# Scores and weighted values for two steps at a time, and a quotient whose clamp and products run on GpSimd

## The chip, the cores and the metric

The kernel runs on one core of one Trainium2 chip. The metric is the device time of one execution in microseconds, from the first instruction to the last, as the median of several runs. Five engines of the core work at the same time, each through its own queue of instructions in order: TensorE (PE, matrix products, with its weight loads shown apart as PEld), VectorE (DVE), ScalarE (ACT), GpSimd (POOL) and SyncE (SP, which here only issues DMAs). They meet at semaphores: an instruction at the head of a queue waits there until what it needs is done, and everything behind it waits too. TensorE writes its results into PSUM, of which this kernel lays out eight banks of 512 fp32 values in each of 128 partitions; DVE and ACT read them from there, and in this kernel GpSimd reads and writes SBUF only.

## The reference, cut to what matters

All data is fp32: an input `x` of eight images of 256 channels and 64 by 64 pixels goes through two layers, each added to its own input after a group normalisation.

Layer 0 makes from each pixel's neighbourhood a small hidden vector (1x1 products `w1`, `w2`, a ReLU, `cw1`, a ReLU), from that nine weights per pixel and group (`cw2`), and sums nine shifted copies of the 1x1 product `x3` with them:

```
h = relu(_bn(concatenate([x1, x2u]), ...)); h = relu(_bn(_conv1x1(h, cw1), ...))
w = _conv1x1(h, cw2, cb2).reshape(B, G, K * K, H, W)
out = einsum('bgskhw,bgkhw->bgshw', x3u, w)
```

Layer 1 adds two branches. The first is local attention in four heads: each pixel's query meets the keys of a 7 by 7 window, softmax, and a sum of the values. The second passes the input through two depthwise 3 by 3 convolutions with a ReLU between them, and multiplies it with a sum over nine softmax weights:

```
att = softmax(einsum('bdn,bdkn->bnk', q, uk + upe)); out_att = einsum('bnk,bdkn->bdn', att, uv)
wts = softmax(einsum('oc,bchw->bohw', Wfc, x).reshape(b, C, 9, h, w), axis=2)
out_conv = sum(oc * wts, over the nine)
return rate1 * out_att + rate2 * out_conv
```

Since `oc` is the same for all nine (the same image is convolved nine times), the second branch is `oc` times a quotient. The kernel computes eight exponentials of differences to the ninth and their sum S, clamps t = min(1 + S, 1e37), and takes t times 1 / t.

## The kernel before, in words

**Tiling.** Work goes in bands of 8 rows (512 pixels, `BAND`); 8 bands make an image, 64 bands the input. The main loop runs over g, the band of layer 1, from -12 to 63. Layer 0 runs `AHEAD` = 12 bands ahead in the same loop, so for g < 0 it stands alone (`alone`), and in the last twelve bands layer 1 does. A band has eight steps s: two halves of the channels (`ct`) times four column blocks of 16 pixels (`m`).

**One step of layer 1.** In the order of the program: `score_tile` takes a PSUM tile of two banks (`sco`, one buffer). `weighted_values` (L747) multiplies the probabilities of the step before last with the values, 16 small matmuls of 112 rows by 64 columns, into columns 256 to 383 of the tile's first bank. `scores` (L703) makes the scores of this step, 8 small matmuls of 64 by 64, and DVE adds the mask and takes the maximum (L712). `add_values` (L757) adds the weighted values to the output rows `xr`. `transposed` (L735) transposes the probabilities of the step before through TensorE, and ACT copies them to SBUF (L737). `exponentials` (L720, ACT) and `probabilities` (L727 DVE, L729 ACT) finish this step's softmax. Two `branch_weights` (L825) each make a 128 by 512 product and its exponential (L830, ACT) into a tile `ex` of two halves, and GpSimd adds the tiles of a half-band (L1026). Between them stand the taps of the depthwise convolutions on DVE (L782, L808), and the queries, keys, values and value transposes of coming bands.

**The quotient.** After step 3 of a half-band `dynamic_sum` runs: GpSimd adds the two halves of the last `ex` (L838), five places later DVE clamps the sum (L845) and takes the reciprocal of its first half (L846), three places later of the second (L850), two places later GpSimd multiplies the sum by it, `oc` by that, and adds to `xr` (L855 to L857). The sum lives in the last `ex` tile, of which there are three.

**Layer 0 in the loop.** `small_maps` (L328) makes the small products at step 0, `value_maps` (L369) the large ones, `hidden_maps` the hidden vector (L429) and `tap_weights` (L447) the nine weights, three at a time after steps 1, 3 and 5. Each weight gives a product over 128 by 1040 on DVE (L460) and a sum on GpSimd (L468).

**What sets the order.** The order on each queue is written by hand: the tile framework records instructions as the Python program reaches them. `advance()` counts places, six to a step, and `after(n, f)` runs f n places later. What waits for what follows from the tiles: an instruction waits for the writers of what it reads, and for the readers of the buffer that it overwrites. All PSUM tiles but `sco` (two banks) and `acc` (one bank) turn in one ring `gen` of five banks: products of L825, L369, L637, L658, L563, L607, L735, L447, L429 and L328 take a bank each in the order of the program.

Of the kernel before, what the change touches and what calls it, by code (L numbers as in the profile page):

```python
# [10 lines left out]
F32 = mybir.dt.float32  # L11
# [7 lines left out]
P = 128  # L19
# [20 lines left out]
TG = 3  # L40
# [25 lines left out]
TAPS_AT = (1, 3, 5), (0, 2, 4)  # L66
PRODUCTS_AT = ((1, 2, 7), (1, 2, 5), (1, 2, 7)), ((7, 14, 10), (9, 17, 13), (12, 20, 16))
# [19 lines left out]
def conv_layers_kernel(ctx: ExitStack, tc: tile.TileContext, ins: dict, out: bass.AP):  # L87
# [98 lines left out]
    def layer1_loads():  # L186


        last = w1.tile([P, NCT, 1, C], F32, tag="rec", name="last", bufs=1)
# [35 lines left out]
    def gn_affine(sts, means, name, done):  # L225
# [9 lines left out]
        def group_means(v, k):  # L235
            pg = ps.tile([P, n], F32, name=f"pg_{name}_{k}", tag="gen", bufs=5)
            nc.tensor.matmul(pg, means, v, start=True, stop=True)
            return pg
# [49 lines left out]
    def scaled_weights(b):  # L288
# [3 lines left out]
        def scale(sc, bi):  # L292
            im.w12s = w0.tile([P, NCT, 2 * REL], F32, tag="w12s", name=f"w12s_{b}", bufs=1)
            im.w3s = w0.tile([P, NCT, C], F32, tag="w3s", name=f"w3s_{b}", bufs=1)
            for kt in range(NCT):
                nc.vector.tensor_scalar(im.w12s[:, kt], w12[:, kt], sc[:, kt : kt + 1], None, ALU.mult)
                nc.vector.tensor_scalar(im.w3s[:, kt], w3[:, kt], sc[:, kt : kt + 1], None, ALU.mult)
            after(5, lambda: through(bi))

        def through(bi):  # L300
            pb = ps.tile([P, 1 + NCT], F32, tag="gen", name=f"pb_{b}", bufs=5)
# [18 lines left out]
    def small_maps(b, i):  # L320
# [4 lines left out]
        p12 = ps.tile([P, R // 2, W], F32, tag="gen", name=f"p12_{b}_{i}", bufs=5)  # L325
# [36 lines left out]
    def value_maps(b, i, mt):  # L362
# [4 lines left out]
        p3 = ps.tile([P, BAND], F32, tag="gen", name=f"p3_{b}_{i}_{mt}", bufs=5)  # L367
# [41 lines left out]
    def hidden_maps(b, i, at):  # L409
# [3 lines left out]
        hids = []  # L413

# [8 lines left out]
        def conv(first, last):  # L423
            if first == 0:
                im.ph = ps.tile([P, SR, W], F32, tag="gen", name=f"ph_{b}_{i}", bufs=5)
            for t in range(first, last):
                n = P if t == 0 else 96
                for q in range(NQR):
                    nc.tensor.matmul(  # L429
                        im.ph[q * REL : (q + 1) * REL], c1[:n, t], hids[t][:n, q * SR : (q + 1) * SR],  # L430
                        start=(t == 0), stop=(t == 2),
                    )

        def relu():
            nc.scalar.activation(h2n[i % 2][:, :, :W], im.ph, AF.Relu, bias=bn2b, scale=bn2s)

        hidden(0)
        for n, f in zip(at, (lambda: hidden(1), lambda: conv(0, 2), lambda: hidden(2), lambda: conv(2, 3), relu)):
            after(n, f)

    def tap_weights(b, i, u, alone, at):
# [3 lines left out]
        pw = ps.tile([P, TG, SR * HP], F32, tag="gen", name=f"pw_{b}_{i}_{u}", bufs=5)  # L445
        for j in range(TG):
            nc.tensor.matmul(  # L447
                pw[:, j], c2[:, TG * u + j], h2n[i % 2].rearrange("p r c -> p (r c)"), start=True, stop=True
            )

        def product(j):
            k = TG * u + j
            if alone and j == TG - 1:
# [11 lines left out]
            if alone and j == TG - 1:  # L465
# [11 lines left out]
        def gather(prod):  # L477
            if u == 0:
                im.part = score_tile(f"sum_{b}_{i}").rearrange("p t (s r c) -> p t s r c", r=SR, c=W)
            for t in range(2):  # L480
                nc.tensor.matmul(
                    im.part[:, t], ident, rows(prod)[:, t * SHARE // 2 : (t + 1) * SHARE // 2],
                    start=(u == 0), stop=(u == KK // TG - 1),
# [18 lines left out]
        for j, n in enumerate(at):  # L502
            after(n, lambda j=j: product(j))


    def norm_rows(b):
# [9 lines left out]
        def by_channel(both):  # L516
            pg = ps.tile([P, NCT, 2], F32, tag="gen", name=f"pgc_{b}", bufs=5)
# [33 lines left out]
    def values(b, j, ct):  # L551
# [3 lines left out]
        pv = ps.tile([P, R, W], F32, tag="gen", name=f"pv_{b}_{j}_{ct}", bufs=5)  # L555
# [45 lines left out]
    def value_tile(b, j, u):  # L601
        im = images[b]
        n = min(R, WP - j * R) * KW
        pvt = ps.tile([CHUNK, 2, C], F32, tag="gen", name=f"pvt_{b}_{j}_{u}", bufs=5)
# [22 lines left out]
    def queries(b, i, ct):  # L627
# [7 lines left out]
        pq = ps.tile([P, R, W], F32, tag="gen", name=f"pq_{nm}", bufs=5)  # L635
# [10 lines left out]
    def keys(b, i, ct):  # L646
# [7 lines left out]
        for a in range(first, last, R):  # L654
            n = min(R, last - a)
            pk = ps.tile([P, R, W], F32, tag="gen", name=f"pk_{b}_{i}_{ct}_{a}", bufs=5)
# [37 lines left out]
    def scores(b, i, ct, m, sco):  # L694
# [4 lines left out]
        nm = f"{b}_{i}_{ct}_{m}"  # L699
        for t in range(2):  # L700
            for h in range(2):
                c0 = (2 * m + t) * TQ
                nc.tensor.matmul(  # L703
                    sco[half[t], h, :NKEY], qb[half[h], 2 * m + t].rearrange("p r c -> p (r c)"),
                    kb[half[h], :, c0 : c0 + KW], start=True, stop=True,
                )

# [422 lines left out]
```

## Time and profile before

| | |
|---|---|
| median of 3 runs | 4155.27 us (4154.16 to 4160.41) |
| the profiled execution | 4152.64 us, its span 4150.9 us |
| TensorE busy | 4022.6 us, 97% of the span |
| DVE, ACT, GpSimd busy | 3591.9, 3081.0 and 2923.0 us |
| first L825 product, last one's end | 247 us and 4137 us |
| mean granted TensorE clock | 0.993 of full |

A group of a profile is a line of the program on one engine, with tiles as out<-in, the shape, the number of instructions, then the busy time and the mean of one in ns, and after the second bar the idle time of the engine just before them and what ended it. A matmul in fp32 is shown as two, and matmuls overlap, since their ends are modelled; what one costs the engine is the distance of two starts. The chain is the work that ended last, followed back step by step to what released it. In the timeline equal instructions in a row are merged: start, length from the first start to the last end, count, and in brackets the idle time ahead with its releaser.

### The profile page before, as it was taken

The page shows a single profiled execution, that of the slowest core. Times are in us where ns is not written, and L with a number is a line of the kernel's source. Part 1 is how long each engine was busy: PE and PEld are TensorE (multiplying, and loading weights), DVE is VectorE, ACT ScalarE, POOL GpSimd, SP SyncE. Part 2 cuts the span into 40 slices and gives each one's busy share as a digit, 9 for nine tenths or more (in the row PEclk, how much of TensorE's full clock was granted, in tenths as well). Part 3 has the DMA queues.
Part 4 walks back from the last instruction along what each step waited for, and adds up shares of the span by engine and source line. Part 5 has one row for each costly group of instructions (what it writes and reads, how often), then busy time and mean ns, then how long its engine had stood idle before and what let it go on. Part 6 is the DMA issues. An engine that isn't in the chain of part 4 may idle for free.

```text
span 4150.9 us, 72735 instructions
## 1 busy us (share of the span) xinstructions
PE 4022.6 (97%) x25292; PEld 2126.8 (51%) x25292; DVE 3591.9 (87%) x7248; ACT 3081.0 (74%) x7726; POOL 2923.0 (70%) x1902
## 2 busy tenths in 40 slices
PE   6789999999999999999999999999999999999998
PEld 3345555555555555555555555555555555455554
DVE  5878998899898898889998898888988889977777
ACT  3467778777787777877778777777778777687776
POOL 4767777677786777777777777777777677744554
PEclk8999999999999999999999999999999999999999
DMA  8854234234244233334234234244233233111100
GB/s 226 194 135 111 73 91 109 72 94 109 62 101 107 76 94 98 81 94 109 72 85 118 72 94 105 66 101 106 71 82 99 65 87 85 33 41 39 39 28 21
DMA packets 381264, 367.89 MB, mean 89 GB/s; under 512 B 55648, under 2 KB 282720, under 8 KB 380640
## 3 DMA queue, kind: packets, MB, share of 16 engines
q1 hardware_dynamic: 377568, 358.68, 34.3%
q8 instruction: 200, 3.28, 0.3%
q10 hardware_dynamic: 3328, 4.55, 0.3%
q14 instruction: 168, 1.38, 0.1%
HBM read 261.42 MB, written 101.71 MB: 87 GB/s over the span
## 4 chain that ended last, share of the span: by engine, by line
PE 71%; DVE 14%; POOL 6%; ACT 5%; DMA 2%; issue 2%; SPq 1%; POOLq 0%; ACTq 0%; DVEq 0%
PE pf L825 33%; PE ptp L735 5%; PE sco L747 5%; PE pk L658 5%; PE sco L703 5%; PE p L369 5%; DVE prod L460 4%; PE pq L637 4%; POOL xg L468 3%; PE pvt L607 2%; PE pv L563 2%; DVE acc L808 2%; PE pw L447 2%; DVE acc L782 2%; POOL ex L1026 2%
## 5 line engine op out<-in xcount | busy, mean ns | idle before, releaser
L825 PE MATMUL pf<-yp,c_wfc 128*128 128x512 f32 x4096 | 1930.5, 595 | 10.6 <-ACT vc L581 5.0
L468 POOL TENSOR_TENSOR xg<-xg,prod 128x1024 f32<-128x1024 f32 x549 | 1203.9, 2193 | 96.6 <-DVE prod L460 64.1
L825 PEld LDWEIGHTS pf<-yp,c_wfc 128*128 128x128 f32 x4096 | 729.9, 190 | 690.5 <-issue 619.4
L1026 POOL TENSOR_TENSOR ex<-ex,ex 128x1024 f32<-128x1024 f32 x384 | 907.7, 2364 | 61.9 <-ACT ex L830 57.2
L830 ACT ACTIVATE ex<-pf 128x512 f32<-128x512 f32 x1024 | 607.3, 593 | 297.9 <-POOL ex L1026 141.3
L782 DVE SCALAR_TENSOR_TENSOR acc<-yp,c_chan,acc 128x504 f32<-128x504 f32 (+3 forms) x1104 | 766.2, 694 | 42.3 <-ACT acc L773 21.7
L460 DVE SCALAR_TENSOR_TENSOR prod<-pw,c_par,x3q 128x1040 f32<-128x1040 f32 x576 | 733.9, 1281 | 66.8 <-PE pw L447 21.6
L808 DVE SCALAR_TENSOR_TENSOR acc<-hid,c_chan,acc 128x504 f32<-128x504 f32 (+3 forms) x1024 | 757.8, 740 | 20.2 <-ACT acc L802 2.1
L855 POOL TENSOR_TENSOR ex<-ex,rec 128x512 f32<-128x512 f32 x127 | 162.3, 1278 | 809.5 <-DVE rec L850 767.1
L729 ACT ACTIVATE prob<-prob,tot 128x196 f32<-128x196 f32 x1024 | 411.6, 450 | 387.2 <-DVE tot L727 386.4
L712 DVE CUSTOM_DVE_ANT_0 prob<-sco,c_mask 128x196 f32<-128x196 f32 x1024 | 325.5, 355 | 272.4 <-PE sco L703 272.0
L720 ACT ACTIVATE prob<-prob,nmax 128x196 f32<-128x196 f32 x1024 | 461.4, 454 | 46.9 <-DVE nmax L712 45.3
L747 PEld LDWEIGHTS sco<-pt,vt 112*64 112x64 f32 x8160 | 283.8, 137 | 182.3 <-issue 51.7
L737 ACT COPY pt<-ptp 112x512 f32<-112x512 f32 x511 | 297.0, 581 | 105.0 <-PE ptp L735 103.0
L735 PE MATMUL ptp<-ident,prob 128*112 128x128 f32 x2044 | 341.7, 287 | 31.2 <-ACT prob L729 30.5
L747 PE MATMUL sco<-pt,vt 112*64 112x64 f32 x8160 | 347.0, 227 | 0.0
L735 PEld LDWEIGHTS ptp<-ident,prob 128*112 128x112 f32 x2044 | 203.9, 133 | 201.4 <-issue 77.7
L703 PE MATMUL sco<-kb,qb 64*64 64x196 f32 x4096 | 295.2, 357 | 0.0
L563 PE MATMUL pv<-yp,c_wv 128*128 128x512 f32 (+2 forms) x576 | 247.3, 554 | 0.6
L369 PE MATMUL p<-xc,w3s 128*128 128x512 f32 x512 | 244.4, 601 | 0.0
L658 PE MATMUL pk<-yp,c_wk 128*128 128x512 f32 (+2 forms) x576 | 240.8, 545 | 0.0
L637 PE MATMUL pq<-yp,c_wq 128*128 128x512 f32 x512 | 240.6, 592 | 0.0
(140 smaller groups left out, 5294.0 us busy)
## 6 DMA issues: line engine op xcount, KB each, us to landing
x<-x3n SPq DMA_DIRECT2D x128, 264.0 KB, 2.1
x3q<-x SPq DMA_DIRECT2D x128, 264.0 KB, 7.2
xc<-in_x SPq DMA_DIRECT2D x64, 512.0 KB, 5.0
xg<-in_x SPq DMA_DIRECT2D x256, 128.0 KB, 4.8
x<-xg SPq DMA_DIRECT2D x256, 128.0 KB, 2.4
yp<-x SPq DMA_DIRECT2D x128, 256.0 KB, 3.3
xr<-x SPq DMA_DIRECT2D x64, 512.0 KB, 5.8
out_x<-xr SPq DMA_DIRECT2D x64, 512.0 KB, 3.1
```

Of the source, the lines that this page charges most:

```text
L369: nc.tensor.matmul(p3, im.w3s[:, kt, mt * P : (mt + 1) * P], im.xc[i][:, kt, :], start=(kt == 0), stop=(kt == NCT - 1),)
L460: nc.vector.scalar_tensor_tensor(prod[:, :, :RUN], pw[:, j, :RUN].unsqueeze(1).to_broadcast([P, SHARE, RUN]), par[:, PCB2 + k : PCB2 + k + 1],
L468: nc.gpsimd.tensor_add(im.xg[i], im.xg[i], rows(prod))
L703: nc.tensor.matmul(sco[half[t], h, :NKEY], qb[half[h], 2 * m + t].rearrange("p r c -> p (r c)"), kb[half[h], :, c0 : c0 + KW], start=True, ...
L720: nc.scalar.activation(prob[:, h, :NKEY], prob[:, h, :NKEY], AF.Exp, bias=nmax[:, h : h + 1], scale=-1.0, accum_out=tot[:, h : h + 1],)
L735: nc.tensor.transpose(ptp[:, h, ch], prob[:, h, ch * CHUNK : (ch + 1) * CHUNK], ident)
L747: nc.tensor.matmul(po[half[h], :, t * TQ : (t + 1) * TQ], im.vt[i + ch, m][:n, t, (2 * ct + h) * HD : (2 * ct + h + 1) * HD], pt[:n, h, ch ...
L782: nc.vector.scalar_tensor_tensor(o, yp[:, ct, ra + dr : rb + dr, ca + dc : cb + dc], chan[:, ct, CW1 + k : CW1 + k + 1], o, ALU.mult, ALU.add,
L808: nc.vector.scalar_tensor_tensor(o, hid[:, ra + dr : rb + dr, ca + dc : cb + dc], chan[:, ct, CW2 + k : CW2 + k + 1], o, ALU.mult, ALU.add,)
L825: nc.tensor.matmul(pf, wfc[:, kt, 2 * m + j, ct * P : (ct + 1) * P], images[b].yp[i][:, kt, PAD : PAD + R], start=(kt == 0), stop=(kt == N ...
L830: nc.scalar.activation(ex[:, j].rearrange("p (r c) -> p r c", r=R), pf, AF.Exp)
L1026: after(4, lambda ex=ex, exb=exb: nc.gpsimd.tensor_add(ex, ex, exb))
```

## The change

The change has five parts.

1. `gen` shrinks from five banks to four. The freed bank is a tile `small` of its own with one buffer. It takes the weighted values of two steps (columns 0 to 255), and in its other half the results of `small_maps` and of the hidden vector.
2. Scores and weighted values are made in every second step, for two steps: 16 score matmuls into a `sco` tile that holds both steps side by side, then up to 32 matmuls of weighted values, then the small products if there are any, then the transposes. In the odd step only the transposes remain; they stand after the first L825 product. `masked` is the part of `scores` that runs on DVE, once in each step as before; the two `add_values` come together.
3. While layer 1 runs, `tap_weights` makes two weights at a time, after steps 1 to 5, and the DVE products follow one and two places later. Before, the third product of a group came seven places later.
4. While layer 1 runs, the hidden vector is summed in two pieces: the first sum is copied to SBUF by ACT in step 4, the second added by DVE in step 6, and then the ReLU. When layer 0 stands alone the sum stays in PSUM, in the bank `acc`.
5. In `dynamic_sum` the sum has a tile of its own, and GpSimd does the clamp. The reciprocal is taken in halves at places 7 and 11, into a tile of half the size, and GpSimd multiplies each half one place later; the rest follows at place 13.

```diff
-TG = 3
+TG = 2, 3
...
-TAPS_AT = (1, 3, 5), (0, 2, 4)
-PRODUCTS_AT = ((1, 2, 7), (1, 2, 5), (1, 2, 7)), ((7, 14, 10), (9, 17, 13), (12, 20, 16))
+TAPS_AT = (1, 2, 3, 4, 5), (0, 2, 4)
+PRODUCTS_AT = ((1, 2),) * 5, ((7, 14, 10), (9, 17, 13), (12, 20, 16))
...
-        p12 = ps.tile([P, R // 2, W], F32, tag="gen", name=f"p12_{b}_{i}", bufs=5)
+        p12 = home[:, 2 * P :].rearrange("p (r c) -> p r c", r=R // 2)
...
+        def one(home):
+            ph = conv(home, 0, 2, 0, 1)
+            after(1, lambda: hidden(2))
+            after(2, lambda: nc.scalar.copy(h2, ph))
+
+        def two(home):
+            ph = conv(home, 2, 3, 2, 2)
+            after(1, lambda: nc.vector.tensor_add(h2, ph, h2))
+            after(3, lambda: relu(h2))
...
-        pw = ps.tile([P, TG, SR * HP], F32, tag="gen", name=f"pw_{b}_{i}_{u}", bufs=5)
-        for j in range(TG):
+        first, n = TG[alone] * u, min(TG[alone], KK - TG[alone] * u)
+        pw = ps.tile([P, n, SR * HP], F32, tag="gen", name=f"pw_{b}_{i}_{u}", bufs=4)
+        for j in range(n):
...
+    def score_of(sco, h, m):
+        return sco[:, h, m % 2 * NKEY : (m % 2 + 1) * NKEY]
...
-        po = sco[:, 0, 256 : 256 + 2 * NQ].rearrange("p (r c) -> p r c", r=R)
+        po = po[:, m % 2]
...
+    def small_tile(nm):
+        return ps.tile([P, 4 * P], F32, tag="small", name=f"small_{nm}")
+
+    def weigh_steps(steps, home):
+        po = home[:, : 2 * P].rearrange("p (s r c) -> p s r c", s=2, r=R)
+        return [(a, weighted_values(*a, pt, po)) for a, pt in steps]
...
-        tot = ex[:, 1]
+        tot = w1.tile([P, BAND], F32, tag="tots", name=f"tot_{b}_{i}_{ct}", bufs=1)
...
-        engine.tensor_add(tot, tot, ex[:, 0])
-        rec = w1.tile([P, BAND], F32, tag="rec", name=f"rec_{b}_{i}_{ct}", bufs=1)
-        n = BAND // 2
-
-        def quotient():
-            nc.vector.tensor_scalar(tot, tot, 1.0, 1.0e37, ALU.add, ALU.min)
-            nc.vector.reciprocal(rec[:, :n], tot[:, :n])
-            after(3, second)
-
-        def second():
-            nc.vector.reciprocal(rec[:, n:], tot[:, n:])
-            after(2, weigh)
+        engine.tensor_add(tot, ex[:, 1], ex[:, 0])
+        engine.tensor_scalar(tot, tot, 1.0, 1.0e37, ALU.add, ALU.min)
+        rec = w1.tile([P, BAND // 2], F32, tag="rec", name=f"rec_{b}_{i}_{ct}", bufs=1)
+
+        def quotient(u):
+            v = tot[:, u * BAND // 2 : (u + 1) * BAND // 2]
+            nc.vector.reciprocal(rec, v)
+            after(1, lambda: engine.tensor_mul(v, v, rec))
...
-            engine.tensor_mul(tot, tot, rec)
             engine.tensor_mul(oc, oc, tot)
...
-        after(5, quotient)
+        after(7, lambda: quotient(0))
+        after(11, lambda: quotient(1))
+        after(13, weigh)
...
-                    sco = score_tile(nm)
-                    weighted = [(a, weighted_values(*a, pt, sco)) for a, pt in pending]
-                    prob, nmax = scores(b, i, ct, m, sco)
+                    weighted = []
+                    if m % 2 == 0:
+                        sco = score_tile(nm)
+                        for e in range(2):
+                            scores(b, i, ct, m + e, sco)
+                        small = small_tile(nm)
+                        weighted, pending = weigh_steps(pending, small), []
+                        if s == 0 and g + AHEAD < B * NB:
+                            mid.append(small_maps(*divmod(g + AHEAD, NB), small))
+                        if s in (4, 6) and convs:
+                            convs.pop()(small)
+                        if before is not None:
+                            pending.append((before[:-1], transposed(nm, before[-1])))
+                    prob, nmax = masked(nm, m, sco)
                     for a, po in weighted:
                         add_values(*a, po)
-                    pending = [] if before is None else [(before[:-1], transposed(nm, before[-1]))]
                     tot = exponentials(nm, prob, nmax)
                 advance()
                 if g >= 0:
                     ex, exb = w1.tile([P, 2, BAND], F32, tag="ex", name=f"ex_{nm}", bufs=3), ex if m else None
                     branch_weights(b, i, ct, m, 0, ex)
+                    if m % 2:
+                        pending.append((before[:-1], transposed(nm, before[-1])))
```

All other tiles of the ring have `bufs=4` in place of `bufs=5`. The tile that takes the last ninth of the `wfc` weights at the start uses the buffers of `oc` in place of those of `rec`.

## The prediction, made before the changed kernel ran

> **What bounds the kernel now.** First the page: busy time, and the chain that ended last.
>
> ```profile
> PE 4022.6 (97%) x25292; PEld 2126.8 (51%) x25292; DVE 3591.9 (87%) x7248; ACT 3081.0 (74%) x7726; POOL 2923.0 (70%) x1902
> ...
> PE 71%; DVE 14%; POOL 6%; ACT 5%; DMA 2%; issue 2%; SPq 1%; POOLq 0%; ACTq 0%; DVEq 0%
> ```
>
> TensorE carries most of the chain, but 97% busy isn't 97% at its rate. So I took the distances of starts. Four matmuls of 512 columns take 1.72 us (0.429 each). Summing such medians per group over the main loop (247 to 4137 us), I find about 140 us of TensorE time above a normal pass. About half are waits of over 0.15 us; the rest is small variation. In a common band (61.6 us; there are 64 bands, those that start an image take 68.8) 59.5 us are work at its normal pitch, 2.1 are lost. That is all that removing waits can win.
>
> The rest must come from the work. The timeline of TensorE in one step:
>
> ```profile
> 2004.92 1.88 PE L369 MATMUL p<-xc,w3s 128*128 128x512 f32 x4
> 2006.73 0.69 PE L747 MATMUL sco<-pt,vt 112*64 112x64 f32 x16
> 2007.34 0.58 PE L703 MATMUL sco<-kb,qb 64*64 64x196 f32 x8
> 2007.85 0.65 PE L735 MATMUL ptp<-ident,prob 128*112 128x128 f32 x4
> 2008.34 1.88 PE L825 MATMUL pf<-yp,c_wfc 128*128 128x512 f32 x4
> ```
>
> L369 should hand over at 2004.92 + 1.72 = 2006.64; L747 starts at 2006.73. By the starts of the single matmuls, a pair of L747 takes 0.0585 us, the first one 0.106; four of L703 take 0.226; the transposes 0.109 each. So a step loses 0.094 entering L747, 0.048 in its first pair, 0.101 going to L703, 0.054 going back to full width: 0.297 us, eight times a band, with nobody to wait for.
>
> Then the waits. A common band stalls at its end; the timelines of TensorE and DVE and the chain of that stretch:
>
> ```profile
> 2053.44 0.78 PE L735 MATMUL ptp<-ident,prob 128*112 128x128 f32 x4 [0.34 <-ACT prob L729]
> ```
> ```profile
> 2008.82 0.41 DVE L845 TENSOR_SCALAR ex<-ex 128x512 f32<-128x512 f32 x1
> ...
> 2039.47 2.38 DVE L845 TENSOR_SCALAR ex<-ex 128x512 f32<-128x512 f32 x1 [0.43 <-POOL ex L838]
> ```
> ```profile
> 2048.14 1.20 DVE prod L460
> ...
> 2052.92 0.81 ACT prob L729 x2
> 2053.73 0.58 ACT qb L641
> 2054.32 0.04 issue
> 2054.36 1.98 PE pf L825 x4
> ```
>
> TensorE waits for a bank and a probability, both behind ACT, behind DVE, which is late. One DVE clamp took 2.38 us beside GpSimd's L468 (2039.39 for 2.17 us), and 0.41 with GpSimd idle.
>
> **What the Trainium skill says.** "TensorEngine Tiling (Array Packing)", Key Properties: changing the tiling mode drains TensorE, changing the tile doesn't. The trace agrees: 0.05 to 0.1 us at each change of shape above, none between transposes and L825. "SBUF — State Buffer", Who interferes with whom: a `tensor_scalar` of DVE in its two-port mode and a GpSimd operation exclude each other for a whole instruction. The 2.38 against 0.41 us fit. "GPSIMD Engine Reference", Elementwise — side-by-side cycle accounting: short bodies with one input take 1.03 cycles per element there, with two inputs about 2.6. In the trace a GpSimd copy of 420 columns takes 534 ns, an addition of 512 1272 ns.
>
> **The change part by part.** *Pairs.* Two steps cost 2 x (0.297 + 0.468 + 0.452 + 0.049 + 0.437) = 3.41 us before (eight pairs of L747, two fours of L703, the first transpose's 0.049 extra, four transposes). Afterwards: changes once, 0.297; scores 4 x 0.226 = 0.904; values 16 x 0.0585 = 0.936; transposes 0.049 + 2 x 0.437 = 0.923; sum 3.06. The odd step's transposes stand between full-width products, so they change no mode. Gain 0.345 us per pair, four pairs, 64 bands: **-88 us**. The small products keep their changes: they leave from full width and come to narrow before, the reverse after. I didn't see scores follow full width in a steady band, so a change may cost 0.05 or 0.12: -60 to -105. Matmul counts are unchanged (the nine weights are nine twice 0.113 either way).
>
> *The wait for scores.* DVE's L712 waits 272.0 us for L703 over the run. In odd steps its scores are there. This idle time isn't TensorE's; it lets DVE start early, which counts below.
>
> *Clamp and halves.* DVE loses 128 x 1070 ns = 137 us, and gains 53 small additions of 128 by 128 (0.3 us as L757, 16 us). GpSimd gains 127 clamps; from the copy's 1.27 ns per column 0.65 us (from 0.44, an estimate by that page's 1.03 cycles at its 1.2 GHz, to 1.27 as the addition): 83 us, and some 0.1 us per quotient for the split: 13 us. GpSimd is then at 3020 us, 74%: not full, but not even over a band. ACT gains 53 copies of 0.3 us, inside its idle time.
>
> *The new waits.* The second reciprocal overwrites the first's tile, so DVE waits for GpSimd's first half product; the first waits for the clamp. I followed GpSimd's new queue with its pitches (L468 2.15, L1026 2.35, L838 1.23, oc 1.35, xr 1.23, kb 0.5, pe 1.1) from the start of step 2, t = 0. The first product ends 1.2, the second 5.4 (behind a reciprocal). From there GpSimd never rests: L468, L1026, a half product, kb, oc, xr to 13.7; two L468 and L1026 to 20.3; two L468 and L1026 to 27.0; the quotient's sum 28.2, its clamp 28.9; two L468 and `pe` 34.3; the half product 34.9. DVE, by its own pitches (product 1.21, mask pair 0.57, reciprocal 1.67, tap 0.72), would be at the first reciprocal at 27.4, so it waits 1.5; the second reciprocal, after taps, a product and masks, would start at 34.3 and waits 0.7. Then 1.67, 0.3 and two taps later the softmax reciprocal ends 38.5, ACT's scaling 39.3, and the query copy (0.57) frees the bank. TensorE, by the pitches above, wants the transposes of step 7 at 39.2 and gets bank and data near 39.9: a stall of 0.7, and perhaps 0.4 at the next bank. That is the 0.85 of before (0.41 + 0.44) plus up to 0.3. The rest of DVE's day is lighter, and the transposes are due 1 to 2 us later in a step.
>
> *Four banks.* The ring loses one, but three tenants go (the small products, hidden vector twice), and a group of weights holds its bank two places, not seven. The closest call is the second L825 of step 3, due at 12.1, whose bank DVE frees at 11.4 with its second product of that step; that of step 5 has 0.9 us. Hidden unless DVE is 0.7 us later; at 1.2 us later about 0.5 us in two places of 52 bands, 52 us.
>
> *Longer hold of `xr`.* The store moves from place 16 to 19 of the quotient, half a step, and the load of the next `xr` follows in step 5 on SP, its first use in step 2: hidden by some 20 us. The stretch before 247 us keeps its order but for the bank of the hidden vector: 0, -5 to +5. The last 14 us: +0.2.
>
> Sum: -88, stalls +15 (0.3 x 51 bands): **-73 us**. Against the profiled execution, 4152.6 - 73 = 4079.6; the median of the runs stands 2.6 higher, so **4082 us**.
>
> **The rivals.** *GpSimd sets the pace* (slower). Place: step 6, DVE's second reciprocal behind GpSimd's half product, behind two L468 and `pe`. It decides when that chain pushes TensorE 1.7 us per band beyond today's stall: 88 us / 52 bands. My walk leaves 1.4 us of room. For it: GpSimd runs without rest for 30 us, and a clamp at 1.27 us adds 0.6 at once. Against: GpSimd's order up to the clamp is nearly that of before, and transposes are due later. At 2.5 us per band: 4155 + 0.8 x 52, about 4195.
>
> *The banks eat it.* 52 us at the two close places, and a little at others: 4125 to 4150. For it: two of four banks wait for DVE, which is 90% busy. Against: pressure in steps 2 to 6 was no smaller before, with a bank held over a full step.
>
> *DVE's relief is worth more.* Without locked clamps and with scores ready early, the common band loses its 0.85 stall and images' first bands (4.3 lost) half: -88 - 0.85 x 51 - 15, about 4015 to 4040. For it: the 2.38 us stood right ahead of the stall. Against: the waits on GpSimd take their place.
>
> *No effect.* Drains could depend on the weights loaded, not on the change of mode: then 4145 to 4160.
>
> **How the numbers follow.** 4082 with 4050 to 4115 as its own range: 0.56. Banks or part of them, 4115 to 4147: 0.14. Relief, below 4050: 0.08. No effect (within 0.2%, 8.3 us, about what a measurement of this kernel can tell): 0.06. Slower: 0.16. Faster 0.78. To hold 8 in 10 the range takes in the relief and the banks: 4032 to 4158.
>
> **What would show it.** Right: blocks of 16 score and 32 value matmuls (L721 and L770 by the new numbering), TensorE's pure pitch per common band near 58.1 us, band time near 60.4; no DVE `tensor_scalar` over 128 by 512, DVE busy near 3470, GpSimd near 3020; the wait of L712 for scores much below 272 us; waits of DVE's reciprocals for GpSimd, 1 to 3 us per band. Wrong: TensorE idle ahead of L857 (the old L825) or the transposes of over 2.5 us a band (GpSimd, if released by scaling late behind a reciprocal; banks, if released by a product), or a block of 16 scores that takes over 1.0 us.

## The result: 1.5% slower, and the profile after

The changed kernel takes 4218.01 us (median; 4217.34 to 4222.56) against 4155.05 us: a ratio of 1.0152, 95% interval 1.014 to 1.0165. The profiled execution took 4217.92 us, its span is 4216.1 us. The page, busy time and shares of the chain:

```profile
PE 3954.1 (94%) x25292; PEld 2135.1 (51%) x25292; DVE 3438.7 (82%) x7143; ACT 3093.7 (73%) x7811; POOL 3170.9 (75%) x2156
...
PE 40%; POOL 32%; DVE 10%; ACT 8%; issue 7%; DMA 2%; SPq 1%; POOLq 0%; ACTq 0%; DVEq 0%
```

TensorE's busy time fell by 68 us, and yet it left the chain: 71% before, 40% now. GpSimd came into it: 6% before, 32% now. Below I split the main loop (first `branch_weights` product to the end of the last) as the prediction did, by distances of TensorE's starts: the normal pitch of every group (the distance that it keeps when nothing holds it), and the time above it.

| main loop, us | before | after |
|---|---|---|
| length | 3890 | 3952 |
| time above the normal pitch | 142 | 319 |
| normal pitch (the difference) | 3748 | 3633 |
| common band: pitch + time above | 59.5 + 2.1 | 57.8 + 5.1 |

So the pairs did gain, some 115 us, and new stalls took some 177. Depending on which distance of a group is taken as normal, the 142 of the kernel before come out between 130 and 154, so both differences are sure to about 12 us. TensorE's timeline in an even step, then at the two places of a common band where it now stands still:

```profile
2060.55 0.92 PE L721 MATMUL sco<-kb,qb 64*64 64x196 f32 x16
2061.40 1.15 PE L770 MATMUL small<-pt,vt 112*64 112x64 f32 x32
2062.49 0.65 PE L758 MATMUL ptp<-ident,prob 128*112 128x128 f32 x4
2062.97 1.88 PE L857 MATMUL pf<-yp,c_wfc 128*128 128x512 f32 x4
...
2088.53 1.99 PE L857 MATMUL pf<-yp,c_wfc 128*128 128x512 f32 x4 [1.17 <-ACT ex L862]
...
2102.92 0.65 PE L758 MATMUL ptp<-ident,prob 128*112 128x128 f32 x4 [2.00 <-ACT qb L660]
```

16 scores start 0.85 us before the values, 32 value matmuls 1.09 us before the transposes: the pair of steps costs 0.85 + 1.09 + 0.48 + 0.44 (the odd step's transposes) = 2.86 us, and 2.95 with the 0.09 us that the change of shape ahead of the scores takes. Then the stalls: 1.17 us at the second L857 of step 5, for a bank that ACT's exponential frees late, and 2.00 us at the transposes of step 7. Who holds ACT and DVE there, by their timelines:

```profile
2087.88 0.60 ACT L862 ACTIVATE ex<-pf 128x512 f32<-128x512 f32 x1 [1.69 <-POOL ex L1071]
```
```profile
2091.23 1.75 DVE L878 RECIPROCAL rec<-tot 128x256 f32<-128x256 f32 x1 [2.85 <-POOL tot L873]
...
2098.04 1.75 DVE L878 RECIPROCAL rec<-tot 128x256 f32<-128x256 f32 x1 [1.40 <-POOL tot L879]
```

Each time it is GpSimd: its sum of exponentials (L1071) for ACT, its clamp (L873) and its half product (L879) for DVE. Between the second reciprocal and the transposes of step 7 stand DVE's taps and softmax reciprocal (to 2101.45) and ACT's scaling and query copy (to 2102.87), which frees the bank. Over the whole run the chain of waits has (who waited for whom: us in total, times, longest):

```profile
DVE rec L878 <- POOL tot L873: 127.3, 54, 3.1
...
ACT ex L862 <- POOL ex L1071: 98.7, 76, 2.0
...
PE ptp L758 <- ACT qb L660: 51.7, 36, 2.0
DVE rec L878 <- POOL tot L879: 48.7, 54, 1.4
DVE prob L735 <- PE sco L721: 34.8, 39, 2.7
PE pf L857 <- ACT ex L862: 34.7, 29, 1.7
```

In the kernel before, GpSimd's quotient product (L855) waited for DVE, and ACT's exponential (L830) for GpSimd's sum (L1026):

```profile
POOL ex L855 <- DVE rec L850: 767.1, 119, 15.4
...
ACT ex L830 <- POOL ex L1026: 141.3, 98, 2.0
...
POOL xg L468 <- DVE prod L460: 64.1, 32, 10.9
```

So ACT waited longer for the sum of exponentials before than it does now (141.3 against 98.7 us). What is new is that TensorE feels it: with five banks it stood 10.6 us ahead of its L825 in the whole run, for whatever reason, and now ACT's exponential alone holds it for 34.7 us there.

And the groups of GpSimd that matter (busy us, mean ns, idle before):

```profile
L487 POOL TENSOR_TENSOR xg<-xg,prod 128x1024 f32<-128x1024 f32 x549 | 1200.7, 2187 | 313.7 <-DVE prod L479 263.5 <-DMA x<-x3n 16.7 <-DMA xs<-in_x 7.7
L1071 POOL TENSOR_TENSOR ex<-ex,ex 128x1024 f32<-128x1024 f32 x384 | 907.4, 2363 | 116.3 <-ACT ex L862 113.4
L873 POOL TENSOR_SCALAR tot<-tot 128x512 f32<-128x512 f32 x127 | 243.6, 1918 | 11.1
...
L870 POOL TENSOR_TENSOR tot<-ex 128x512 f32<-128x512 f32 x127 | 161.3, 1270 | 10.0
L652 POOL COPY kb<-kb 128x420 f32<-128x420 f32 x112 | 59.8, 534 | 0.1
```

A clamp on GpSimd takes 1.918 us, three times the 0.65 that the prediction took and more than its upper end of 1.27. GpSimd also sits idle for 263.5 us ahead of the sums of layer 0 (L487), waiting for DVE's products; the kernel before had 64.1 us of that. This is not more idle time, but other idle time: ahead of the quotient it fell from 767.1 to 302.3 us (L879), and in all from 1228 to 1045 us.

### The profile page after: what moved, and what is told of

It reads as the page before. It is cut to its first block, busy times and chain, and to the rows that moved or that the text cites. A ratio compares the mean times of both kernels' runs of the same rounds, so it can differ in the third digit from the quotient of the medians.

```text
span 4216.1 us, 72848 instructions
## 1 busy us (share of the span) xinstructions
PE 3954.1 (94%) x25292; PEld 2135.1 (51%) x25292; DVE 3438.7 (82%) x7143; ACT 3093.7 (73%) x7811; POOL 3170.9 (75%) x2156
## 4 chain that ended last, share of the span: by engine, by line
PE 40%; POOL 32%; DVE 10%; ACT 8%; issue 7%; DMA 2%; SPq 1%; POOLq 0%; ACTq 0%; DVEq 0%
PE pf L857 18%; POOL xg L487 16%; POOL ex L1071 7%; PE p L369 4%; PE small L770 3%; PE pk L677 3%; PE sco L721 3%; DVE acc L840 3%; PE ptp L758 2%; DVE prod L479 2%; DVE rec L878 2%; POOL tot L873 2%; PE pvt L626 2%; POOL tot L879 2%; PE pq L656 2%
## 5 line engine op out<-in xcount | busy, mean ns | idle before, releaser
L857 PE MATMUL pf<-yp,c_wfc 128*128 128x512 f32 x4096 | 1932.9, 596 | 39.4 <-ACT ex L862 34.7
L487 POOL TENSOR_TENSOR xg<-xg,prod 128x1024 f32<-128x1024 f32 x549 | 1200.7, 2187 | 313.7 <-DVE prod L479 263.5
L857 PEld LDWEIGHTS pf<-yp,c_wfc 128*128 128x128 f32 x4096 | 732.7, 191 | 751.1 <-issue 633.7
L1071 POOL TENSOR_TENSOR ex<-ex,ex 128x1024 f32<-128x1024 f32 x384 | 907.4, 2363 | 116.3 <-ACT ex L862 113.4
L878 DVE RECIPROCAL rec<-tot 128x256 f32<-128x256 f32 x256 | 446.5, 1744 | 176.0 <-POOL tot L873 127.3
L879 POOL TENSOR_TENSOR tot<-tot,rec 128x256 f32<-128x256 f32 x254 | 185.0, 728 | 302.4 <-DVE rec L878 302.3
L758 PE MATMUL ptp<-ident,prob 128*112 128x128 f32 x2044 | 322.1, 280 | 66.2 <-ACT qb L660 51.7
L758 PEld LDWEIGHTS ptp<-ident,prob 128*112 128x112 f32 x2044 | 222.2, 133 | 268.2 <-issue 94.9
L735 DVE CUSTOM_DVE_ANT_0 prob<-sco,c_mask 128x196 f32<-128x196 f32 x1024 | 325.0, 355 | 37.8 <-PE sco L721 34.8
L770 PEld LDWEIGHTS small<-pt,vt 112*64 112x64 f32 x8144 | 258.1, 138 | 75.9 <-issue 75.9
L770 PE MATMUL small<-pt,vt 112*64 112x64 f32 x8144 | 293.4, 225 | 0.0
L750 DVE RECIPROCAL tot<-tot 128x2 f32<-128x2 f32 x512 | 82.4, 161 | 240.6 <-ACT prob L743 239.0
L677 PE MATMUL pk<-yp,c_wk 128*128 128x512 f32 (+2 forms) x576 | 250.0, 562 | 7.6 <-ACT ex L862 7.5
```

The costliest lines, as they stand in the source:

```text
L487: nc.gpsimd.tensor_add(im.xg[i], im.xg[i], rows(prod))
L758: nc.tensor.transpose(ptp[:, h, ch], prob[:, h, ch * CHUNK : (ch + 1) * CHUNK], ident)
L770: nc.tensor.matmul(po[half[h], :, t * TQ : (t + 1) * TQ], im.vt[i + ch, m][:n, t, (2 * ct + h) * HD : (2 * ct + h + 1) * HD], pt[:n, h, ch ...
L857: nc.tensor.matmul(pf, wfc[:, kt, 2 * m + j, ct * P : (ct + 1) * P], images[b].yp[i][:, kt, PAD : PAD + R], start=(kt == 0), stop=(kt == N ...
L878: nc.vector.reciprocal(rec, v)
L1071: after(4, lambda ex=ex, exb=exb: nc.gpsimd.tensor_add(ex, ex, exb))
```

## The experiments

Ratios are to the kernel before on the same chip, whose median lies between 4154.55 and 4155.51 us. Three theories stood at the start or came up on the way. **G**: GpSimd is late, with the clamp the new load on it. **B**: the ring of four banks has no slack, whoever is late. **C**, formed later: GpSimd does its work in the wrong order, the sum of exponentials behind sums of layer 0 that aren't ready.

Four of the runs must be read with care, since TensorE's mean granted clock is lower in them than the 0.992 of the changed kernel: 0.970 with part 5 undone, 0.984 with the weights by threes, 0.980 with the first half's quotient later, 0.972 with the reciprocals at the old places. An estimate of what that can cost at most, the difference of the clocks times the span, is 95, 34, 51 and 86 us. Their times hold this as well as the waits named below; why the clock is lower there was not tested.

### Parts of the change on their own

**Part 5 undone**, all of `dynamic_sum` as before (the limit on DVE in the `ex` tile, a full `rec`, products at the old place).

> The changed kernel with its fifth part undone: the sum stays in the last exponentials' tile, DVE clamps it and takes both reciprocals without waiting for GpSimd. Theory G (the clamp of 1.92 us on GpSimd and the waits of both reciprocals for GpSimd make the loss): TensorE keeps its saving of 1.7 us a band and the stalls fall back to about 2 us a band, so 4050 to 4100 us. Theory B (the ring of four banks and the weights two at a time make the loss): the stalls stay near 5 us a band, 4180 us or more.

Measured: 4331.39 us, 1.0426 (1.0409 to 1.0444). Theory G missed. The time lies in B's open range, but the longest wait of DVE is one that neither theory names:

```profile
DVE xr L789 <- POOL xr L889: 275.3, 127, 3.6
```

By the order of the program the old quotient makes GpSimd's addition to `xr` earlier, and the two `add_values` of a pair, now together, wait for it on DVE. So it isn't a clean undo, and decides nothing between G and B.

**No clamp**: the changed kernel without L873.

```diff
-        engine.tensor_scalar(tot, tot, 1.0, 1.0e37, ALU.add, ALU.min)
```

> The changed kernel without the clamp, neither on GpSimd nor on DVE (1 + S and the limit are left out, so the quotient is S times 1/S); the halves and their waits stay. Theory G, and the clamp is the larger part of it: 3.8 us of GpSimd per band go, the first reciprocal's wait of 2.9 us falls below 1, 4070 to 4120 us. If the halves' wait is the larger part: 4150 to 4190. Theory B: 4200 or more.

Measured: 4115.03 us, 0.9906 (0.9891 to 0.992), 103 us under the changed kernel. 127 clamps of 1.92 us are 244 us, so 0.42 us of time per us of clamp. As theory G had it, in its upper end. The stall at step 5 is untouched (by starts 43 us, 40 of them in 29 bands, with or without the clamp; PE waits 34.6 us for ACT's exponential there), the one ahead of the transposes after L857 falls from 79 to 19 us. So G holds for step 7, and something else makes step 5.

**Part 5 alone** on the kernel before.

```diff
-        engine.tensor_add(tot, tot, ex[:, 0])
+        engine.tensor_add(tot, ex[:, 1], ex[:, 0])
+        engine.tensor_scalar(tot, tot, 1.0, 1.0e37, ALU.add, ALU.min)
...
-        after(5, quotient)
+        after(7, lambda: quotient(0))
+        after(11, lambda: quotient(1))
+        after(13, weigh)
```

> The kernel before with the fifth part alone (sum in its own tile, clamp on GpSimd, quotient by halves). Theory G: slower than before by 40 to 120 us, 4195 to 4275, with DVE's reciprocals waiting for GpSimd. Theory B: no slower, 4120 to 4160, since DVE loses a clamp of 1.07 us.

Measured: 4145.46 us, 0.9979 (0.997 to 0.9988). As theory B had it. The same clamp on GpSimd shows no harm here, though DVE's reciprocal waits for it just as long:

```profile
DVE rec L846 <- POOL tot L841: 120.8, 51, 4.4
```

So G can't be all: the wait for the clamp is in both kernels, and this one is still 9 us faster than the kernel before.

**The smaller ring alone**: the kernel before with four banks in `gen`, its small products still in the ring.

```diff
-bufs=5)
+bufs=4)
```

> The kernel before with a ring of four banks in place of five, and nothing else. Theory B: 60 us or more slower, 4215 or more. Theory G says nothing on it; since this kernel holds more tiles in the ring than the changed one, it bounds what a bank costs from above: I expect 4170 to 4230.

Measured: 4241.59 us, 1.0211 (1.0196 to 1.0226): 87 us, as theory B had it, and 12 over the upper end that I gave. This kernel has no bank to give. But here the small products and the hidden vector still turn in the ring, which the change took out, so it doesn't measure part 1 in the changed kernel, and no run gives that kernel a fifth bank for its ring: its tiles fill all eight.

**Part 3 undone**: weights of layer 0 by threes in the changed kernel.

```diff
-TG = 2, 3
+TG = 3, 3
...
-TAPS_AT = (1, 2, 3, 4, 5), (0, 2, 4)
-PRODUCTS_AT = ((1, 2),) * 5, (
+TAPS_AT = (1, 3, 5), (0, 2, 4)
+PRODUCTS_AT = ((1, 2, 7), (1, 2, 5), (1, 2, 7)), (
```

> The changed kernel with part 3 undone: the weights of layer 0 three at a time after steps 1, 3 and 5, with the third product of a group 5 or 7 places later, as in the kernel before. GpSimd then has one sum of layer 0 less ahead of the sum of exponentials in step 3 and ahead of the quotient's. Theory P (part 3 put the sums ahead): 4110 to 4170. Against: a group of three holds one of four banks for seven places, and DVE gets its products in lumps: 4220 or more.

Measured: 4242.74 us, 1.0212 (1.0196 to 1.0227), 25 us over the changed kernel: a loss, which the second reading had expected, though the lower clock alone could be as much. Its longest TensorE wait:

```profile
PE pf L857 <- ACT qb L660: 112.2, 54, 3.7
```

The wait has moved from the transposes to a bank that the query copy frees. By the order of the program a group of three holds its bank for seven places, which would explain it; shown is only that taking part 3 back on its own gains nothing in this kernel. Theory P, that part 3 put the sums ahead of the exponentials and so made the loss, is not borne out: GpSimd even waits 417.1 us for DVE's products here.

### The clamp and the reciprocal's tile

**Clamp on DVE**, ahead of the first reciprocal.

```diff
-        engine.tensor_scalar(tot, tot, 1.0, 1.0e37, ALU.add, ALU.min)
...
+            if u == 0:
+                nc.vector.tensor_scalar(tot, tot, 1.0, 1.0e37, ALU.add, ALU.min)
             nc.vector.reciprocal(rec, v)
```

> The changed kernel with one line moved: DVE makes the clamp of the whole sum, right ahead of its first reciprocal, in place of GpSimd behind the sum. All else stays. Theory G (the clamp on GpSimd, 1.92 us in a stretch in which GpSimd never rests, is what the change lost): GpSimd's busy time falls by some 240 us to about 2930, DVE's rises by 0.4 to 1.5 us per clamp (52 to 190 us), and the time falls by half or more of the 103 us that leaving the clamp out gave: 4120 to 4170. Theory B (a ring of four banks has no slack, whoever is late): DVE's late clamp costs as much as GpSimd's did: 4190 to 4230.

Measured: 4171.52 us, 1.0041 (1.0027 to 1.0055), 46 us under the changed kernel and 1.5 over the range of theory G. DVE's clamp has a mean of 1069 ns.

**Whole reciprocal tile.**

```diff
-        rec = w1.tile([P, BAND // 2], F32, tag="rec", name=f"rec_{b}_{i}_{ct}", bufs=1)
+        rec = w1.tile([P, BAND], F32, tag="rec", name=f"rec_{b}_{i}_{ct}", bufs=1)
...
-            nc.vector.reciprocal(rec, v)
-            after(1, lambda: engine.tensor_mul(v, v, rec))
+            r = rec[:, u * BAND // 2 : (u + 1) * BAND // 2]
+            nc.vector.reciprocal(r, v)
+            after(1, lambda: engine.tensor_mul(v, v, r))
```

> The changed kernel with the reciprocal's tile at full size again, so that the second half's reciprocal no longer overwrites what GpSimd's first half product reads. The wait of the reciprocal for that product (48.7 us) goes. Theory G1 (the clamp alone): that wait had slack, 4195 to 4218. Theory G2 (the small tile is the path by which GpSimd's lateness reaches DVE): at least 50 us less, 4150 to 4170, and the wait of the first reciprocal for the clamp stays near 127 us in both.

Measured: 4160.44 us, 1.0014 (1.0007 to 1.0021): 58 us for a wait of 48.7, as G2 had it. Its waits, DVE's and then TensorE's:

```profile
DVE rec L879 <- POOL tot L873: 127.0, 54, 3.1
...
PE ptp L758 <- ACT qb L660: 15.0, 29, 0.6
```

The first reciprocal waits as long as ever; without the second one's wait the transposes of step 7 stand 15.0 us instead of 51.7. The order of events from step 6 on is what the prediction's walk and its first rival named: half product, second reciprocal, softmax, query copy, bank.

**Both.**

> Both single repairs at once: DVE makes the clamp (alone 4171.5, 47 us under the changed kernel) and the reciprocal's tile is whole (alone 4160.4, 58 under). If they heal two different stalls the gains add up: 4105 to 4125. If both only make DVE less late ahead of the same stall, the transposes of step 7, they overlap: with the clamp on DVE the second reciprocal hardly waits for GpSimd any more, so the whole tile adds little and the time is 4155 to 4171.

Measured: 4170.83 us, 1.0039 (1.0024 to 1.0054), as with the DVE clamp alone. They overlap: both mend the same stall. TensorE's wait for the query copy is 31.1 us with the clamp on DVE, 30.5 with both, 15.0 with the whole tile alone.

**The clamp twice.**

```diff
         engine.tensor_scalar(tot, tot, 1.0, 1.0e37, ALU.add, ALU.min)
+        engine.tensor_scalar(tot, tot, 0.0, 1.0e37, ALU.add, ALU.min)
```

> The changed kernel with the clamp on GpSimd made twice over (the second adds 0 and limits again). Theory G (GpSimd sets the pace in this kernel): 127 more instructions of 1.92 us, 244 us, of which as in the first dose some 40% or more reach the end: 4300 to 4460, the first reciprocal's wait for the clamp grows from 127 by at least 100 us. Theory B (banks alone, GpSimd's load is not the cause): 4215 to 4240.

Measured: 4338.9 us, 1.0447 (1.0431 to 1.0462), 121 us more for another 243 us: 0.50 per us. As theory G had it. The waits grow at step 7 above all:

```profile
DVE rec L879 <- POOL tot L874: 236.3, 56, 5.1
PE ptp L758 <- ACT qb L660: 103.2, 42, 3.2
ACT ex L862 <- POOL ex L1072: 99.1, 76, 2.0
...
PE pf L857 <- ACT ex L862: 34.7, 29, 1.7
```

From none to two clamps the time climbs by 103 and 121 us. The step 5 stall (last two lines) doesn't feel it: it is a second cause.

**First half's quotient six places later.**

```diff
+        d = 0 if ct else 6
+        after(d, lambda: engine.tensor_scalar(tot, tot, 1.0, 1.0e37, ALU.add, ALU.min))
+        after(7 + d, lambda: quotient(0))
+        after(11 + d, lambda: quotient(1))
+        after(13 + d, weigh)
```

> The changed kernel with the same work, but for the first half of the channels the clamp, both halves of the quotient and the products with it come six places (one step) later; the second half's stay. Theory G as a matter of place (the clamp stands in front of two sums of layer 0 and a half product in a stretch without rest): the first reciprocal of half the cases finds its clamp long done, waits of the reciprocals for GpSimd fall from 176 to under 100 us, and the time to 4140 to 4185. Theory of load (GpSimd has 240 us more work, wherever it stands): 4205 to 4230.

Measured: 4291.02 us, 1.0331 (1.0316 to 1.0346): both missed. TensorE's waits show the new one:

```profile
PE sco L721 <- DVE kb L692: 106.8, 42, 3.4
```

The scores of the next band wait for DVE's part of the keys. That the two long reciprocals now stand ahead of them on DVE's queue is read from the order of the program; no run tests it.

**Reciprocals at the old places 5 and 8**, clamp on DVE, whole tile.

```diff
-        after(7, lambda: quotient(0))
-        after(11, lambda: quotient(1))
+        after(5, lambda: quotient(0))
+        after(8, lambda: quotient(1))
```

> As the run with both repairs (clamp on DVE, whole tile), and the two reciprocals at places 5 and 8, as in the kernel before, in place of 7 and 11; the products of GpSimd with oc and xr stay at place 13. Theory of place (DVE is late at step 7 since the second reciprocal stands half a step later than before): 30 us or more under the run with both repairs, about 4110 to 4140, and the stall between the second L857 of step 6 and the transposes of step 7 shrinks. Theory of load (DVE's work in front of step 7 is the same, only its order differs): within 10 us of the run with both repairs.

Measured: 4315.25 us, 1.0386 (1.0368 to 1.0403). Neither reading: 144 us worse than at 7 and 11. DVE's and TensorE's waits:

```profile
DVE tot L879 <- POOL tot L870: 101.5, 54, 3.8
```
```profile
PE ptp L758 <- ACT prob L752: 104.4, 36, 3.9
```

DVE now comes to the quotient before GpSimd's sum is there, and stands. This and the step 5 stall point to the same: GpSimd's exponentials are late, whether it has the clamp or not.

### The order on GpSimd

In the timeline of GpSimd of the changed kernel (the band of the stalls above), the sum of exponentials stands behind two sums of layer 0 in each step, and the first of these wait for DVE:

```profile
2062.04 2.20 POOL L487 TENSOR_TENSOR xg<-xg,prod 128x1024 f32<-128x1024 f32 x1 [2.09 <-DVE prod L479]
2066.14 2.18 POOL L487 TENSOR_TENSOR xg<-xg,prod 128x1024 f32<-128x1024 f32 x1 [1.90 <-DVE prod L479]
2068.27 2.38 POOL L1071 TENSOR_TENSOR ex<-ex,ex 128x1024 f32<-128x1024 f32 x1
...
2081.09 4.45 POOL L487 TENSOR_TENSOR xg<-xg,prod 128x1024 f32<-128x1024 f32 x2
2085.50 2.35 POOL L1071 TENSOR_TENSOR ex<-ex,ex 128x1024 f32<-128x1024 f32 x1
2087.93 1.26 POOL L870 TENSOR_TENSOR tot<-ex 128x512 f32<-128x512 f32 x1
2089.28 1.92 POOL L873 TENSOR_SCALAR tot<-tot 128x512 f32<-128x512 f32 x1
```

Theory C: move L1071 ahead of them, and GpSimd adds exponentials while DVE makes the products.

```diff
-                        after(4, lambda ex=ex, exb=exb: nc.gpsimd.tensor_add(ex, ex, exb))
+                        after(2, lambda ex=ex, exb=exb: nc.gpsimd.tensor_add(ex, ex, exb))
```

**On the changed kernel with the whole tile:**

> The changed kernel with the whole reciprocal tile (4160.4), and GpSimd adds the exponentials of two steps (L1071) ahead of the two sums of layer 0 that follow a step, in place of behind them. Theory C (with four banks, TensorE's second L857 of step 5 waits 1.3 us in 29 bands for a bank that ACT frees late, since ACT's exponential waits for an ex tile, and that for GpSimd's L1071 behind two sums of 2.2 us): the stall of 43 us at that place goes, 4117 to 4130. If another tenant of the ring is late there as well, or the sums of layer 0 are then late for DVE: 4150 to 4175.

Measured: 4070.55 us, 0.9795 (0.9781 to 0.981), below both readings: 90 us under the whole tile alone, more than the 43 of the step 5 stall. Its page:

```profile
PE 3929.7 (97%) x25292; PEld 2138.3 (53%) x25292; DVE 3434.7 (84%) x7143; ACT 3092.9 (76%) x7811; POOL 3172.3 (78%) x2156
...
PE 75%; POOL 7%; DVE 6%; ACT 6%; issue 3%; DMA 2%; SPq 1%; ACTq 0%; DVEq 0%; POOLq 0%
```

GpSimd does the same 3172 us of work, clamps included, and is off the chain.

**With the clamp on DVE as well:**

> Clamp on DVE, whole reciprocal tile, and the sum of exponentials ahead of the sums of layer 0. By theory C this is 30 to 43 us under the run with both repairs alone; with the pure work of TensorE 109 us under the kernel before, anything below 4145 beats both kernels and the one with part 5 alone.

Measured: 4100.31 us, 0.987 (0.9855 to 0.9884): 71 us under the run with both repairs, where 30 to 43 were expected, and 30 us worse than with the clamp on GpSimd: once GpSimd is in order, the clamp is better there, as the change has it.

**That edit alone on the changed kernel:**

> The changed kernel with a single edit: GpSimd's L1071 two places earlier, ahead of the two sums of layer 0. Theory C1 (the order on GpSimd is the cause; clamp and small reciprocal tile hurt only because GpSimd came to them late): 4070 to 4095. Theory C2 (two separate stalls, at step 5 by the bank and at step 7 by the small tile): the step 5 stall of 43 us and little more goes, 4140 to 4175.

Measured: 4105.45 us, 0.9878 (0.9864 to 0.9893), 113 us under the changed kernel, 10 over the range of C1 and 35 under that of C2. Its GpSimd in the same band, then DVE's waits:

```profile
2004.86 2.39 POOL L1071 TENSOR_TENSOR ex<-ex,ex 128x1024 f32<-128x1024 f32 x1 [0.93 <-ACT ex L862]
2007.20 2.18 POOL L487 TENSOR_TENSOR xg<-xg,prod 128x1024 f32<-128x1024 f32 x1
2010.11 2.17 POOL L487 TENSOR_TENSOR xg<-xg,prod 128x1024 f32<-128x1024 f32 x1 [0.72 <-DVE prod L479]
...
2029.45 1.27 POOL L870 TENSOR_TENSOR tot<-ex 128x512 f32<-128x512 f32 x1
2030.81 1.92 POOL L873 TENSOR_SCALAR tot<-tot 128x512 f32<-128x512 f32 x1
```
```profile
DVE rec L878 <- POOL tot L879: 33.1, 35, 1.4
...
DVE rec L878 <- POOL tot L873: 16.2, 35, 0.6
```

Idle time at the head of GpSimd's queue falls from 2.09 + 1.90 to 0.93 + 0.72 us. The band starts at 2047.63 us in the changed kernel and 1991.61 here (first L857), so the clamp ends 43.6 us and 41.1 us after it: 2.5 us earlier, of which the missing idle time is 2.3. ACT's waits for L1071 and TensorE's for ACT's exponential (98.7 and 34.7 us) are gone from the list, the first reciprocal's falls from 127.3 to 16.2 us. The small tile's is still 33.1, and the whole tile takes it: 35 us, to 4070.55.

**The same edit on the kernel before:**

> The kernel before, with the same edit on its sum of exponentials (L1026 two places earlier). If the lateness is made by the change (two sums of layer 0 after each step, a ring of four banks): within 10 us of 4155. If the sum of exponentials was late in the kernel before as well (its wait of ACT for L1026 is 141.3 us there): 4115 to 4140, and the gain of the changed kernel with the edit must be read against that.

Measured: 4176.58 us, 1.005 (1.0035 to 1.0065), 22 us slower, outside both. DVE's longest wait, 12.8 us without the edit:

```profile
DVE prod L460 <- POOL xg L468: 212.4, 117, 2.6
```

There the sums of layer 0 are then what comes late. So the same order is the better one in the old kernel and the worse one in the changed one. Which part of the change turned it no run shows.

**The edit, without the clamp:**

> The changed kernel with the sum of exponentials ahead, and without the clamp (it leaves out 1 + S and the limit). Without the edit, leaving the clamp out gave 103 us. Theory C1: with GpSimd on time the clamp has cover, and leaving it out gives under 30 us against the run with the edit alone. Theory G (GpSimd's load sets the pace): again 80 us or more.

Measured: 4051.23 us, 0.9748 (0.9732 to 0.9764). Leaving the clamp out is now worth 54 us instead of 103; C1 said under 30, G 80 or more, and neither held. In the new order about half of the clamp's price is gone, not all.

| kernel | us | time above the pitch, main loop |
|---|---|---|
| after | 4218.01 | 319 |
| without clamp | 4115.03 | 217 |
| whole tile | 4160.44 | 261 |
| sum of exponentials earlier | 4105.45 | 203 |
| both of these | 4070.55 | 168 |
| earlier, without clamp | 4051.23 | 155 |

The pitch per common band stays 57.8 us in all six. The two edits together beat the kernel before by 2.05% and the changed one by 3.5% (4070.55 / 4218.01).

## Why the prediction was wrong

The forecast was 4082 us, faster; measured were 4218.01, slower, and outside the range (4032 to 4158). By its own steps:

- **Pairs, -88 us: right, and some 27 us too little.** 3.06 us per pair were 2.95; the normal pitch of the main loop fell by some 115 us, of a common band to 57.8 (forecast 58.1). That the odd step's transposes cost no change of shape held: they start 1.72 us after the L857 ahead of them, and L677 0.44 us after them.
- **The wait for scores: right.** L735 (the old L712) waits 34.8 us, from 272.0.
- **Clamp and halves: the step that failed first.** DVE came out at 3438.7 us (forecast 3470). But the clamp was priced by the copy, 0.65 us, between 0.44 (an estimate from the 1.03 cycles per element of short bodies in the Trainium skill's "GPSIMD Engine Reference", Elementwise — side-by-side cycle accounting) and 1.27 (the addition). Measured 1.918: dearer than the two-input addition, so neither the price nor the bounds held. GpSimd is busy for 3170.9 us, not 3020. The error is 127 x 1.27 = 161 us of work; at the 0.42 to 0.50 us of time per us that none, one and two clamps showed, an estimate of 68 to 80 us of time, about half of the 136 that the forecast was off.
- **The new waits: right in mechanism, wrong in size.** The walk had the first reciprocal wait 1.5 us and the second 0.7; in the profile they wait 2.85 and 1.40, and the difference of the first, 1.35, is the clamp's 1.27 and little else. The walk also left out a fill of 0.53 us (L395) that GpSimd makes ahead of the half product. It said 0.7 us of stall at the transposes of step 7, from the same chain; it is 2.00 in the band shown, 1.57 by starts in the common ones. Rival one (*GpSimd sets the pace*) named place and chain, and said itself that a clamp of 1.27 us would add 0.6 at once. It gave 4195.
- **Four banks, hidden unless DVE is late: failed.** The bank that comes late is in step 5, as feared (0.9 us of slack were given to it), but not by DVE: ACT's exponential frees it, and waits for an `ex` tile that GpSimd has yet to add. 43 us by starts, which stay when the clamp is out and go when L1071 moves. The walk followed GpSimd for what DVE needs of it, and not for what ACT needs; this path was put at nothing without a reason. The rival *the banks eat it* was right that banks come late, but looked for DVE behind them, as the walk did.
- **GpSimd's order: taken as it was.** The walk had two sums of layer 0 ahead of the sum of exponentials in every step, and even the wait of the second for its product (at 5.4); its times for GpSimd fit the profile up to the clamp (from the first of these sums to the end of the quotient's sum 27.0 us, in the profile 27.15). That this order was nearly the old one counted there as a reason against a loss, and no other order was priced. Moving L1071 took back 113 us, more than any other single edit; it overlaps with the clamp and the tile, for which reason the terms don't add up to the miss. GpSimd's idle time ahead of the sums of layer 0 doesn't explain the loss by itself: it is 64.1 us before and 263.5 now, but 358.8 with part 5 alone, which is faster than before.
- **`xr` later, the prologue: right.** No wait of `add_values` for the load of `xr` shows in the main loop. The first L857 starts at 250.0 us against 247.2, inside -5 to +5, and from the end of the last one 14.3 us remain against 13.9.

The stalls were to cost 15 us and cost 177; the pairs gave 27 more than forecast: 4082 + 162 - 27 = 4217. The marks set for being wrong were met: over 2.5 us a band ahead of L857 and the transposes by starts (1.35 + 1.57 in a common band), released by ACT behind GpSimd.

What stays open: which part of the change made the old order the worse one, and what the fifth bank is worth in the changed kernel. Of the clamp's 103 us, 54 remain after the move; the whole tile takes 35 of what the move leaves, but no run left the clamp out with both, so how far these are the same is not settled. Why the stall at the end of an image (band of 65.6 us after, 60.0 before) is larger than in the common band was not followed.

## What to carry to other kernels

When work is moved to an engine whose queue is already long, follow that queue for every engine that waits on it, each with its own due time; here DVE was followed and ACT was not. An instruction that must wait at the head of an in-order queue takes the ready ones behind it along: the same order was the better one by 22 us in one of these kernels and the worse one by 113 us in the other, so after a change of what its neighbours need try the order anew, and not the load alone. And price an operation on an engine by the same instruction there or leave its upper end open: a row with another operation bounds nothing.

## What the runs showed of the hardware

- On GpSimd a TENSOR_SCALAR with two operations (add, min) over 128 by 512 fp32 took 1918 ns, a TENSOR_TENSOR of the same shape 1270, a COPY over 420 columns 534. Of the three the one with one tensor input and two scalars is the dearest.
- The same TENSOR_SCALAR on DVE took 1069 ns in the mean of 128, in the kernel before as in the run with the clamp back on DVE, though it was 0.41 us where GpSimd rested, and 821 ns in the mean with the sum of exponentials moved. Which engine should have it depends on the order around it: at first DVE (4171.52 against 4218.01), with the order mended and the whole tile GpSimd (4070.55 against 4100.31).
